# Two sums for the last three pairs of experts, and the third added earlier: one change to a fused two-layer transformer kernel on Trainium2

## The chip, the cores and the metric

The kernel runs on one core of a Trainium2 chip. The metric is the time of one execution on the device in microseconds (us), as the median of several runs. The engines are called by their short names: PE (TensorE, the matrix products), DVE (VectorE), ACT (ScalarE), POOL (GpSimd) and SP (SyncE, which here only issues DMAs). POOL also issues DMAs, the indirect ones; ACT issues a few. All data is float32.

## The reference, cut to what matters

Two transformer layers work on 2048 tokens of 512 features. Layer 0 is windowed attention and a mixture of 64 experts, of which each token uses 8; layer 1 is another windowed attention and a dense network of 2048 inner features whose weights go through Walsh-Hadamard transforms. The change lies where the experts end and layer 1 begins:

```python
# layer 0, experts: every token's rows of 8 experts are weighted and added up
y = lax.ragged_dot(hact, jnp.swapaxes(down_proj, 1, 2), group_sizes)
out = jnp.zeros_like(x).at[tok].add(y * w[:, None])
...
x = x + gb * _L0_ffn_ref(h, ...)
# layer 1 starts with a normalisation of that x
h = _layernorm(x, axis=-1) * (1 + ca) + sa
x = x + ga * _L1_attn_ref(h, ...)
```

## The kernel before, in words

**Residual and tiles.** The stream `x` stays in SBUF as `x_sb`, 16 tiles of 128 tokens by 512 features. The experts are sorted by load and taken in 32 pairs (`for q in range(NQ)`, L1104); `ROOM` (L44) says how many rows a pair's experts may hold, from 440 down to 184. Rows that do not fit go to a loop of their own behind the last pair (`tc.For_i(0, n_more, 1)`, L1149), which all engines pass, taken or not.

**One pair.** For each pair the rows are gathered by POOL (`fetch_x`, L877), transposed by PE (`x_T`, L886; its results are copied by ACT and DVE), multiplied (`gate_up`, L902, then `down`, L935), and DVE weights the result into a tile `yo` (L950, pool `ex`, 8 buffers). The weights of pair q+2 are fetched by SP while pair q is worked on (`fetch_w`, L612, from L1118).

**Sums.** The rows of an expert belong to scattered tokens. They are added in DRAM: POOL issues an indirect DMA that adds a `yo` tile of up to 128 rows onto a buffer `sums[k]` (`add_rows`, L953). Two DMAs that add onto the same buffer must not overlap, so each waits until the one before it on that buffer has landed. There are six buffers (`NSUM`, L55): the pairs 0 to 20 (up to `LATE`, L56) use the buffers 0, 1, 2 in turn, the pairs 21 to 31 use 3, 4, 5 in turn, by a running number of the add (L967):

```python
k = st_.setdefault("sum", 0)
st_["sum"] += 1
add_rows(k % 3 + (3 if q >= LATE else 0), yo, tidx[0:m, col : col + 1])
```

Over the whole kernel there are 164 adds, numbered 0 to 163 here. The pairs 28 to 31 have four each: pair 28 has the adds 148 to 151, pair 29 152 to 155, pair 30 156 to 159, and pair 31 160 to 163.

**The first three sums.** When the pairs that use them are done, SP loads them back during the pairs 22 to 29 (`earlier`, L971, called at L1110), two token tiles and six loads of 256 KB in each pair, and DVE adds them to `x_sb` one pair later (L1144). They land in buffers of the pools `h1` and `h2` (tags `wdb`, one buffer, and `wda`, two) that other work used before, and `load_proj` (L858) takes the `wda` buffers again in the last pair for layer 1's projections.

**Behind the last pair.** Two column blocks of layer 1's down weights still lack one Hadamard product: `fetch_last` (L1051) loads eight pieces, `last_products` (L1064) multiplies them on PE into the pool `p_x` (two PSUM banks), copies each into a `yo` buffer by ACT and DVE in turn, and stores it to DRAM, the even ones from ACT and the odd ones from SP. `wdo_n` is the copy of product n. Then comes the loop for rows that did not fit, at which every engine waits for all DMAs that were issued before it.

**Layer 1's start.** `rest(i)` (L1219) loads token tile i of the sums 3, 4 and 5 into a buffer (`cb`, three of them), the first two tiles partly from ACT. `summed(i)` (L1248) adds the three to `x_sb` on DVE and takes the statistics, `normal(i)` scales on ACT, and PE transposes (`across`, L1271) and projects. Tiles go in the groups of `GROUPS` (L62): two, two, four, four and four; the work on a group's sums stands between the projections of the group before it.

**What sets the order.** A scheduler of the framework places every engine's instructions; each engine then runs its own list in order, DMA issues on SP and ACT included. `tc.issue_after` (as in `in_turn`, L595) pins some of it by hand. DMAs from SP and ACT share eight completion semaphores in turn, so a DMA also waits until the eighth before it has landed.

Of the kernel before, what the change touches and what calls it, by code (L numbers as in the profile page):

```python
# [12 lines left out]
F32 = mybir.dt.float32  # L13
# [9 lines left out]
P = 128  # L23
T = 2048
NT = T // P
D = 512
# [17 lines left out]
ROOM = (  # L44
    440, 384, 352, 344, 332, 320, 312, 312, 304, 296, 292, 288, 284, 280, 276, 268,
    260, 256, 252, 252, 248, 248, 240, 240, 232, 228, 220, 220, 212, 204, 200, 184,
)
# [5 lines left out]


NSUM = 6  # L55
LATE = 21  # L56
WARM = 6
NX = 12

# [69 lines left out]
def block_kernel(ctx: ExitStack, tc: tile.TileContext, t: dict, out: bass.AP):  # L129
    nc = tc.nc  # L130
# [41 lines left out]
    wd_d = dram.tile([KC, P, FC, P], F32, tag="wd_d", name="wd_d")  # L172
    sums = [dram.tile([T + P, D], F32, tag=f"sum{k}", name=f"sum{k}") for k in range(NSUM)]
# [91 lines left out]
    with tc.tile_pool(name="a0", bufs=1) as ap, tc.tile_pool(name="a0k", bufs=1) as kp:  # L265
# [8 lines left out]
        with tc.tile_pool(name="a0h", bufs=1) as hp, tc.tile_pool(name="a0w", bufs=1) as wp, tc.tile_pool(  # L274
            name="a0n", bufs=5
# [85 lines left out]
            third = TQ // 3  # L361
            for n in range(3):
                normed_T([3 * n, 3 * n + 1, 3 * n + 2], hT, 3 * n * P, m0[1], m0[0], np_, psA, "a0")
                cols = slice(n * third, (n + 1) * third)
                ps = psA.tile([P, D], F32, tag="ps", name=f"k0_{n}")
# [5 lines left out]
                for c in range(KC):  # L371
                    ps = psA.tile([P, D], F32, tag="ps", name=f"q0_{n}_{c}")
# [9 lines left out]
            ps = psA.tile([P, 8, 64], F32, tag="ps", name="v0")  # L382
            ps2 = psA.tile([P, 64], F32, tag="ps", name="v0_8")
            left = TQ - 8 * P
            for i in range(TQT):
                n = P if i < 8 else left
                o = ps[:, i, :] if i < 8 else ps2[0:n, :]
# [5 lines left out]
            n = 0  # L393
# [26 lines left out]
        with tc.tile_pool(name="rn", bufs=4) as rn, tc.tile_pool(name="a0s", bufs=2) as sp, tc.tile_pool(name="p_s", bufs=2, space=PSUM) as p_s, tc.tile_pool(  # L420
            name="p_t", bufs=2, space=PSUM
# [204 lines left out]
    with tc.tile_pool(name="rw", bufs=1) as rw, tc.tile_pool(name="rh", bufs=3) as rh:  # L626
        with tc.tile_pool(name="p_q", bufs=3, space=PSUM) as p_q, tc.tile_pool(
# [158 lines left out]
            n = 0  # L786
# [84 lines left out]
    with tc.tile_pool(name="h1", bufs=1) as h1, tc.tile_pool(name="p_x", bufs=2, space=PSUM) as p_x, tc.tile_pool(  # L871
# [81 lines left out]
        def add_rows(k, yo, idx):  # L953
            G.indirect_dma_start(  # L954
                out=sums[k][:, :],
                out_offset=bass.IndirectOffsetOnAxis(ap=idx, axis=0),
                in_=yo,
                in_offset=None,
                compute_op=ALU.add,
            )  # L960

        def to_sums(q):
            def put(h, b, m, yo):
                col = FIRST[2 * q + h] + b
                k = st_.setdefault("sum", 0)
                st_["sum"] += 1
                add_rows(k % 3 + (3 if q >= LATE else 0), yo, tidx[0:m, col : col + 1])  # L967

            return put

        def earlier(n):  # L971

            got = []
            for i in (2 * n, 2 * n + 1):
                for k in range(3):
                    j, at = divmod(3 * i + k, 4)
                    if at == 0:
                        pool, tag = (h1, "wdb") if j % 3 == 2 else (h2, "wda")
                        st_["sa"] = pool.tile([P, 4, D], F32, tag=tag, name=f"sa_{j}")
                    part = st_["sa"][:, at, :]  # L980
                    nc.sync.dma_start(out=part, in_=sums[k][i * P : (i + 1) * P, :])
                    got.append((i, part))
            return got


# [77 lines left out]

        def last_products(got):  # L1064
            for n, (cb, c4, a) in enumerate(got):
                ps = p_x.tile([P, 4, P], F32, tag="xp", name=f"wdh_{cb}_{c4}")
                with in_turn():
                    st_["pe"] = mm(ps, had, a)
                o = ex.tile([P, D], F32, tag="yo", name=f"wdo_{n}", bufs=8).rearrange("p (c m) -> p c m", c=4)
                (V.tensor_copy if n % 2 else S.copy)(o, ps)  # L1070
                (nc.sync if n % 2 else nc.scalar).dma_start(out=wd_d[cb][:, c4 : c4 + 4, :], in_=o)


        def turn(q):
# [29 lines left out]
        for q in range(NQ):  # L1104
            if q == NQ - 1:
                n_more = nc.values_load(more[0:1, 0:1], min_val=0, max_val=MORE)
            two = [st_[2 * q], st_[2 * q + 1]]
            late = st_.pop("late", [])
            if LATE < q <= LATE + NT // 2:
                st_["late"] = earlier(q - LATE - 1)  # L1110

            def fetch(p):
                for r in (2 * p, 2 * p + 1) if p < NQ else ():
                    fetch_w(r)
                    fetch_x(r)

            if q:
                fetch(q + 2)  # L1118
            if q == NQ - 1:
                load_proj()  # L1120
                behind_it = fetch_last()
            steps = turn(q + 1) if q + 1 < NQ else []
            with in_turn():
                hA, hB, last = gate_up(
                    q, [s["w"][0] for s in two], [s["xT"] for s in two], ROOM[q], lambda: take(steps, 2),
                    lambda: take(opening, KC),
                )
            if q == 0:
                fetch(2)
            take(steps, 2)  # L1130
            if q + 1 < NQ:
                with tc.issue_after(last.ins):
                    shares(q + 1)
            for s in range(0, ROOM[q], P):

                with in_turn(), tc.issue_after(st_["gx"].ins):
                    down(q, s, [a["w"][1] for a in two], hA, hB, ROOM[q], [a["share"] for a in two], to_sums(q))
                take(steps, 2)
            take(steps, 2 * KC)
            with tc.issue_after(last.ins):  # L1140
                for _ in range(2):
                    next(side)
                for i, part in late:
                    V.tensor_tensor(x_sb[:, i, :], x_sb[:, i, :], part, ALU.add)  # L1144
# [47 lines left out]
    with tc.tile_pool(name="a1", bufs=1) as ap:  # L1192
# [7 lines left out]
        with tc.tile_pool(name="b1h", bufs=2) as hp, tc.tile_pool(  # L1200
# [18 lines left out]
            def rest(i, eng=None):  # L1219

                rests[i] = cb.tile([P, 3, D], F32, tag="sum", name=f"sum_{i}")
                for k in range(3):
                    (eng if k and eng else nc.sync).dma_start(
                        out=rests[i][:, k, :], in_=sums[3 + k][i * P : (i + 1) * P, :]
                    )

# [16 lines left out]
            def prepare(g):  # L1243

                first, n = GROUPS[g]
                norms = {}

                def summed(i):  # L1248
                    for k in range(3):
                        v_(V.tensor_tensor, x_sb[:, i, :], x_sb[:, i, :], rests[i][:, k, :], ALU.add)  # L1250
                    if i + 3 < NT:
                        rest(i + 3)
                    st = small.tile([P, 6], F32, tag="st", name=f"st_a1_{i}")
                    mv = small.tile([P, 1, 2], F32, tag="mv", name=f"mv_a1_{i}")
                    v_(V.bn_stats, st, x_sb[:, i, :])
                    v_(V.bn_aggr, mv[:, 0, :], st)
                    rs = small.tile([P, 1], F32, tag="rs", name=f"rs_a1_{i}")
                    S.activation(rs, mv[:, :, 1], AF.Sqrt, bias=eps)
                    norms[i] = mv, rs

                def normal(i):
                    mv, rs = norms[i]
                    v_(V.reciprocal, rs, rs)

                    off = small.tile([P, 1], F32, tag="off", name=f"off_a1_{i}")
                    v_(V.scalar_tensor_tensor, off, mv[:, 0, 0:1], -1.0, rs, ALU.mult, ALU.mult)
                    xn = np_.tile([P, D], F32, tag="xn", name=f"xn_a1_{i}")
                    S.activation(xn, x_sb[:, i, :], AF.Identity, bias=off, scale=rs)
                    norms[i] = xn

                def across():  # L1271
                    hT = hTs[g] = hp.tile([P, KC, D], F32, tag="hT", name=f"hT1_{g}")
                    for c in range(KC):
                        ps = psA.tile([P, D], F32, tag="ps", name=f"nT_a1_{g}_{c}")
                        for a in range(n):
                            with after("PE"):
                                prev["PE"] = TE.transpose(
                                    ps[:, a * P : (a + 1) * P], norms[first + a][:, c * P : (c + 1) * P], ident
                                )
                        o, ps = hT[:, c, 0 : n * P], ps[:, 0 : n * P]  # L1280
                        sc_, sh_ = m1[1][:, c : c + 1], m1[0][:, c : c + 1]
                        if c % 2:
                            S.activation(o, ps, AF.Identity, bias=sh_, scale=sc_)
                        else:
                            v_(V.tensor_scalar, o, ps, sc_, sh_, ALU.mult, ALU.add)

                steps = []
                for i in range(first, first + n + 1):
                    def step(i=i):
                        if i < first + n:  # L1290
                            summed(i)
                        if i > first:
                            normal(i - 1)

                    steps.append(step)
                return steps, across
# [504 lines left out]
```

## Time and profile before

| what | value |
|---|---|
| time, three runs | 2038.03, 2042.15 and 2044.28 us, median 2042.15 us |
| the profiled execution's own time | 2033.98 us |
| its span (first to last instruction) | 2032.2 us |
| PE busy in the span | 1936.8 us (95%) |
| DVE, ACT, POOL busy | 1087.7, 509.8 and 563.7 us |
| PE's idle time between the experts and layer 1 | 17.59 us, from 1031.4 to 1049.0 us |
| mean granted PE clock | 0.98 |

All stamps are microseconds from the start of the span. A line of the timeline has the start, the duration, the engine, the source line, the operation, the tiles written and read, a count, and in brackets how long the engine had been idle before it and what ended that. "L954 POOL DMA_INDIRECT" is the time in which POOL prepares an add, not its travel. The time from that stamp until the data has landed is the landing time; the view of DMAs gives it for a single add when the window holds only that one. In the view that cuts the span into windows, the last two columns are the mean busy share of the DMA engines and what they moved; a share of 1.0 means that they always had work. In the chain of waits, a line "DMA a<-b" is time in which the end was waiting for that transfer.

### The profile page before, as it was taken

How to read it: one execution, taken by the hardware profiler on the slowest of the kernel's cores; microseconds unless marked ns; L12 is line 12 of the kernel's file. 1: busy time of each engine (PE TensorE's matmuls, PEld its weight loads, DVE VectorE, ACT ScalarE, POOL GpSimd, SP SyncE). 2: the span in 40 equal slices, each digit the busy share in tenths (PEclk: the TensorE clock that was granted, in tenths of full speed). 3: DMA queues.
4: the chain of work that ended last, by engine and by line, in shares of the span. 5: the costliest groups of instructions: out<-in, count | busy, mean ns of one | idle time of the engine just before them, and what ended most of it. 6: DMA issues, size and time to landing. Idle time of an engine off the chain costs nothing.

```text
span 2032.2 us, 28791 instructions
## 1 busy us (share of the span) xinstructions
PE 1936.8 (95%) x10794; PEld 1237.7 (61%) x10794; DVE 1087.7 (54%) x2591; ACT 509.8 (25%) x1185; POOL 563.7 (28%) x438
## 2 busy tenths in 40 slices
PE   8999878999999999999968989999999999999998
PEld 4655545455555556666635555556777776777775
DVE  3566564534454443345558767766545545535443
ACT  2333323111111111111111158774111111111101
POOL 1500003575667676566531100110100010010000
PEclk9999968999999999999979999999999999999999
DMA  7790036688889899999974100004111211211210
GB/s 277 290 345 22 32 108 208 156 217 240 202 237 236 216 269 237 267 317 310 314 248 144 52 12 2 2 23 137 51 63 53 72 62 42 83 43 61 83 42 21
DMA packets 123469, 294.50 MB, mean 145 GB/s; under 512 B 21224, under 2 KB 29160, under 8 KB 120768
## 3 DMA queue, kind: packets, MB, share of 16 engines
q1 hardware_dynamic: 85424, 211.32, 30.3%
q0 software_dynamic: 36032, 77.30, 17.8%
q10 hardware_dynamic: 1872, 4.00, 0.5%
q8 instruction: 87, 1.43, 0.3%
q14 instruction: 54, 0.44, 0.1%
HBM read 212.01 MB, written 78.20 MB: 143 GB/s over the span
## 4 chain that ended last, share of the span: by engine, by line
PE 77%; DVE 8%; DMA 5%; ACT 5%; issue 1%; POOL 0%; SPq 0%; ACTq 0%; DVEq 0%; POOLq 0%
PE y L134 20%; PE p L134 18%; PE gu L134 11%; PE gub L134 5%; PE xp L893 4%; PE s L134 3%; ACT pr L1431 3%; PE po L134 2%; PE po_a L134 2%; DMA w<-in_L_gu 2%; PE pt L1376 2%; DVE x_sb L1211 1%; DMA sum<-yo,tidx 1%; PE tps L134 1%; PE o L134 1%
## 5 line engine op out<-in xcount | busy, mean ns | idle before, releaser
L954 POOL DMA_INDIRECT sum<-yo,tidx x164 | 272.3, 1660 | 112.3 <-DMA sum<-yo,tidx 41.5
L608 POOL DMA_INDIRECT xring<-h_d,tidx x164 | 181.7, 1108 | 361.4 <-PE rps L134 229.7
L134 PE MATMUL gu<-xT,w 128*128 128x312 f32 (+26 forms) x1024 | 245.2, 397 | 1.8 <-DMA w<-in_L_gu 1.8
L134 PE MATMUL y<-wd,act 128*128 128x512 f32 x512 | 230.3, 593 | 1.5 <-DVE act L1570 1.4
L134 PEld LDWEIGHTS gu<-xT,w 128*128 128x128 f32 x1024 | 189.8, 191 | 58.0 <-issue 18.3
L134 PEld LDWEIGHTS y<-wd,act 128*128 128x128 f32 x512 | 97.0, 190 | 98.0 <-issue 91.6
L896 ACT ACTIVATE xT<-xp,modc,modc 128x312 f32<-128x312 f32 (+26 forms) x128 | 74.1, 579 | 328.7 <-PE xp L893 300.4
L950 DVE SCALAR_TENSOR_TENSOR yo<-y,wc,modr 128x512 f32<-128x512 f32 (+22 forms) x164 | 116.6, 744 | 69.8 <-PE y L134 69.3
L134 PE MATMUL y<-w,hA 128*128 128x512 f32 (+22 forms) x328 | 149.5, 596 | 0.5 <-DVE yo L950 0.5
L916 DVE TENSOR_TENSOR hA<-hA,gu 128x312 f32<-128x312 f32 (+26 forms) x64 | 28.2, 440 | 189.0 <-PE xp L893 110.3
L1431 ACT ACTIVATE pr<-ng,nb 128x208 f32<-128x208 f32 (+1 forms) x256 | 115.1, 451 | 52.4 <-DVE nb L1421 52.4
L134 PE MATMUL gub<-xT,w 128*64 128x312 f32 (+26 forms) x1024 | 125.4, 398 | 0.0
L237 POOL TENSOR_TENSOR xh<-hT 128x1024 f32<-128x1024 f32 x4 | 9.4, 2361 | 416.9 <-ACT hT L1645 401.7
L134 PE MATMUL p<-xt,ws 128*128 128x256 f32 x512 | 120.9, 379 | 3.5 <-DVE ws L1570 3.5
L134 PE MATMUL p<-xt,wr 128*128 128x256 f32 x512 | 120.8, 379 | 0.0
L893 PEld LDWEIGHTS xp<-cst,xring 128*128 128x128 f32 x656 | 73.0, 142 | 73.0 <-issue 55.8
L134 PE MATMUL p<-xh,wr 128*128 128x256 f32 x512 | 116.6, 379 | 0.3 <-DVE u L1570 0.3
L134 PEld LDWEIGHTS p<-xt,ws 128*128 128x128 f32 x512 | 96.7, 190 | 27.4 <-issue 15.8
L134 PEld LDWEIGHTS p<-xt,wr 128*128 128x128 f32 x512 | 96.8, 190 | 23.6 <-issue 10.8
L893 PE MATMUL xp<-cst,xring 128*128 128x128 f32 x656 | 100.2, 284 | 6.0 <-DMA xring<-h_d,tidx 4.8
L134 PEld LDWEIGHTS p<-xh,wr 128*128 128x128 f32 x512 | 96.9, 190 | 14.3 <-DVE u L1570 0.7
L1725 ACT ACTIVATE sg<-two,L_ws_gate 128x512 f32<-128x512 f32 x32 | 23.1, 721 | 308.8 <-DVE two L1570 308.7
(384 smaller groups left out, 2957.9 us busy)
## 6 DMA issues: line engine op xcount, KB each, us to landing
w<-in_L_gu SPq DMA_DIRECT2D x64, 768.0 KB, 7.6
wr<-in_L_Wug SPq DMA_DIRECT2D x64, 512.0 KB, 4.7
sum<-xring SPq DMA_DIRECT2D x6, 4352.0 KB, 31.0
w<-in_L_dn SPq DMA_DIRECT2D x64, 256.0 KB, 8.9
sa<-sum SPq DMA_DIRECT2D x48, 256.0 KB, 10.2
sum<-sum SPq DMA_DIRECT2D x44, 256.0 KB, 3.6
w<-in_L_dn SPq DMA_DIRECT2D x64, 128.0 KB, 8.9
xring<-in_L_wmod SPq DMA_DIRECT2D x4, 1536.0 KB, 11.3
```

The costliest lines, as they stand in the source:

```text
L134: return TE.matmul(o, lhsT, rhs, start=start, stop=stop)
L237: eng.tensor_tensor(b[:, :, 0, :], a[:, :, 0, :], a[:, :, 1, :], ALU.add)
L608: return G.indirect_dma_start(out=dst, out_offset=None, in_=src[:, :], in_offset=bass.IndirectOffsetOnAxis(ap=idx, axis=0))
L893: st_["pe"] = TE.transpose(xp[:, b * P : (b + 1) * P], xg[:, c * P : (c + 1) * P], ident)
L896: S.activation(xT[:, c, 0:n], xp[:, 0:n], AF.Identity, bias=sh, scale=sc)
L916: V.tensor_tensor(o[:, 0:n], o[:, 0:n], ps[1][:, 0:n], ALU.mult)
L950: V.scalar_tensor_tensor(yo, ys[h], shares[h][rows, b : b + 1], m0[5][rows, :], ALU.mult, ALU.mult)
L954: G.indirect_dma_start(out=sums[k][:, :], out_offset=bass.IndirectOffsetOnAxis(ap=idx, axis=0), in_=yo, in_offset=None, compute_op=ALU.add,)
L1211: prev["V"] = f(*a)
L1376: prev["PE"] = f(*a)
L1431: S.activation(prs[i, c][:, j, :nk], ng[:, :nk], AF.Exp, bias=nb, scale=-1.0, accum_out=totals[i][:, c, j : j + 1],)
L1725: S.activation(sg, gate, AF.Silu, scale=wsg[:, f : f + 1])
```

## The change: a third sum that ends earlier, and five banks

The first three sums end one pair earlier (`LATE` 20 in place of 21): the pairs 0 to 19 use the sums 0 to 2, and their loads and DVE adds fall one pair earlier too. The pairs 20 to 28 use the sums 3, 4, 5 in turn. The pairs 29, 30 and 31 use only 4 and 5 in turn. Sum 3 is thereby complete after pair 28. For the token tiles 0 to 7 (`AHEAD` 8) it is loaded at the start of pair 30 (`third`, eight loads of 256 KB, into the buffers `wdb` and `wda`) and added to `x_sb` in pair 30's list of DVE adds. Layer 1 then loads and adds two sums for the tiles 0 to 7, and three for the tiles 8 to 15 as before. For the tiles 0 and 1 ACT issues one load each in place of two.

The products behind the last pair use the two banks of `p_x` and the three of `p_g` in turn. SP stores only the products 1 and 3; ACT stores the other six.

```diff
-LATE = 21
+LATE = 20
+LAST = len(ROOM) - 3
+AHEAD = 8
...
-                add_rows(k % 3 + (3 if q >= LATE else 0), yo, tidx[0:m, col : col + 1])
+                add_rows(k % 2 + 4 if q >= LAST else k % 3 + (3 if q >= LATE else 0), yo, tidx[0:m, col : col + 1])
...
+        def third():
+
+            got = []
+            for i in range(AHEAD):
+                if i % 4 == 0:
+                    pool, tag = ((h1, "wdb"), (h2, "wda"))[i // 4]
+                    part = pool.tile([P, 4, D], F32, tag=tag, name=f"sc_{i}")
+                nc.sync.dma_start(out=part[:, i % 4, :], in_=sums[3][i * P : (i + 1) * P, :])
+                got.append((i, part[:, i % 4, :]))
+            return got
...
-                ps = p_x.tile([P, 4, P], F32, tag="xp", name=f"wdh_{cb}_{c4}")
+                pool, tag = (p_g, "g") if n % 2 else (p_x, "xp")
+                ps = pool.tile([P, 4, P], F32, tag=tag, name=f"wdh_{cb}_{c4}")
...
-                (nc.sync if n % 2 else nc.scalar).dma_start(out=wd_d[cb][:, c4 : c4 + 4, :], in_=o)
+                (nc.sync if n in (1, 3) else nc.scalar).dma_start(out=wd_d[cb][:, c4 : c4 + 4, :], in_=o)
...
             if LATE < q <= LATE + NT // 2:
                 st_["late"] = earlier(q - LATE - 1)
+            if q == NQ - 2:
+                late = late + third()
...
-                for k in range(3):
-                    (eng if k and eng else nc.sync).dma_start(
+                for k in range(1 if i < AHEAD else 0, 3):
+                    (eng if k == 2 and eng else nc.sync).dma_start(
                         out=rests[i][:, k, :], in_=sums[3 + k][i * P : (i + 1) * P, :]
                     )
...
-                    for k in range(3):
+                    for k in range(1 if i < AHEAD else 0, 3):
                         v_(V.tensor_tensor, x_sb[:, i, :], x_sb[:, i, :], rests[i][:, k, :], ALU.add)
```

## The prediction

> **What bounds the kernel now.** I read the page first. PE is busy for 95% of the span, so the change can only gain where PE stands still. Then PE's timeline around the change: from 840 us, where the loads of the first three sums begin, to the last product, PE idles twice, 0.93 us at 877.89 and 0.89 us at 964.27. The one large hole is between the experts and layer 1: 17.59 us before the first transpose at 1049.01. The third view is the chain of waits through that hole. Columns are start, duration and what was waited for.
>
> ```profile
> 1025.69 5.35 DMA sum<-yo,tidx
> ...
> 1031.14 0.59 ACT wdo L1070
> ...
> 1031.75 3.16 DMA wd_d<-wdo
> ...
> 1035.64 2.22 DMA wd_d<-wdo
> ...
> 1039.23 6.90 DMA sum<-sum
> ...
> 1046.23 0.70 DVE x_sb L1211
> ...
> 1049.72 0.48 PE nT_a L1277
> ```
>
> The hole begins with a scatter add. Add 162, issued by POOL at 1025.69, lands at 1031.04. Only then is its `yo` buffer free for the copy of product 6. That copy is stored (landing 1034.91), all engines pass the loop for rows that did not fit, the last store (product 7, placed behind the loop) lands at 1037.86, and only then do the loads of the sums begin; the last load that the first two token tiles need is issued at 1039.23 and lands at 1046.14. So everything hangs on when add 162 lands. POOL's timeline shows how the adds come along; these are the adds 151 to 163:
>
> ```profile
> 989.10 2.84 POOL L954 DMA_INDIRECT sum<-yo,tidx  x1 [0.86 <-DVE x_sb L1144]
> 992.25 2.68 POOL L954 DMA_INDIRECT sum<-yo,tidx  x1 [0.30 <-DMA sum<-yo,tidx]
> 996.18 1.57 POOL L954 DMA_INDIRECT sum<-yo,tidx  x1 [1.25 <-DVE xT L898]
> 998.36 1.84 POOL L954 DMA_INDIRECT sum<-yo,tidx  x1 [0.62 <-issue]
> 1003.45 1.83 POOL L954 DMA_INDIRECT sum<-yo,tidx  x1 [3.25 <-issue]
> 1007.70 1.57 POOL L954 DMA_INDIRECT sum<-yo,tidx  x1 [2.42 <-DVE yo L950]
> 1009.98 1.57 POOL L954 DMA_INDIRECT sum<-yo,tidx  x1 [0.71 <-DVE x_sb L1144]
> 1014.14 1.51 POOL L954 DMA_INDIRECT sum<-yo,tidx  x1 [2.59 <-DMA sum<-yo,tidx]
> 1016.16 1.53 POOL L954 DMA_INDIRECT sum<-yo,tidx  x1 [0.51 <-DVE hA L916]
> 1021.92 1.59 POOL L954 DMA_INDIRECT sum<-yo,tidx  x1 [4.23 <-DVE yo L950]
> 1023.82 1.57 POOL L954 DMA_INDIRECT sum<-yo,tidx  x1 [0.30 <-issue]
> 1025.69 1.45 POOL L954 DMA_INDIRECT sum<-yo,tidx  x1 [0.30 <-DVE yo L950]
> 1027.52 1.45 POOL L954 DMA_INDIRECT sum<-yo,tidx  x1 [0.38 <-issue]
> ```
>
> The view of DMAs, one add to a window, gives landing times: 8.7 us for add 150 (issued 986.73), 10.3 for the one at 992.25, 8.4 at 996.18, 10.9 at 998.36, 9.9 at 1003.45, 7.6 at 1007.70, 7.9 at 1014.14, then 4.8, 5.6, 5.3 and 5.6 for pair 31. An add starts about 0.8 us after the add three before it has landed: 992.25 + 10.3 = 1002.55, and add 155 starts at 1003.45; 1003.45 + 9.9 = 1013.35, and add 158 starts at 1014.14. So in pairs 29 and 30 the adds are already held by their own landing, and three sums just keep up: three adds in about 11 us, four in 14 to 15, while a pair takes PE some 16 us (its gate products start at 977.97, 994.11 and 1010.09). Why landing takes so long shows in the windows, whose last two columns are the DMA engines' share and GB/s:
>
> ```profile
> 990.00:1000.00 10.00, 10.00 (x54) 7.39 (x52) 5.84 (x11) 1.71 (x4) 7.83 (x4) 1.00 1.06 327
> 1010.00:1020.00 10.00, 10.00 (x73) 8.12 (x73) 2.52 (x6) 1.47 (x4) 4.59 (x3) 1.00 1.05 304
> 1020.00:1030.00 10.00, 10.00 (x26) 2.83 (x24) 4.74 (x7) 1.76 (x3) 6.06 (x4) 1.00 0.95 215
> ```
>
> The DMA engines always have work until 1020; then the load falls, and with it the landing time.
>
> **The two sums.** From pair 29 on, an add waits for the add two before it. The even adds, 152 to 162, become one chain on sum 4, behind add 151, which is on sum 4 too and landed near 997.6 (0.8 before add 154 started). I walk the chain with the landing time of the row nearest in time, and 0.8 us for each turn. Add 152 starts at 998.4 and takes 10.9, landing at 1009.3. Add 154 starts at 1010.1, takes 7.7, lands at 1017.8. Add 156: 1018.6, about 6.3 (between 7.9 at 1014.14 and 4.8 at 1021.92), 1024.9. Add 158: 1025.7, 5.3, 1031.0. Add 160: 1031.8, 5.5, 1037.3. Add 162: 1038.1, 5.5, 1043.6. Before it was 1031.04, so the hole ends **12.6 us** later, since the way from there to the loads (copy, store, loop, last store) is unchanged. The bounds: with every add's own landing time from before (10.3, 10.9, 7.6, 7.9, 4.8, 5.3; together 46.8, and 4.8 of turns) it lands at 1049.2, 18 us later. If instead the landing time is the adds queueing behind each other, two in flight need two thirds of it, not below 4.8: 7.3, 5.2 and four times 4.8, with the turns 36.5, landing at 1034.1, 3 us later.
>
> Here the Trainium skill speaks against my sum, and for the change. "DMA: Bandwidth & Descriptors", section "Anatomy of one DMA — SWDGE (gpsimd) path", gives a DMA issued by GpSimd about 2.0 us plus its bytes over 436 GB/s; that would be an estimated 2.6 us for 256 KB. By it a turn takes 3.4 us, six turns 20.4, the chain would be done before the last `yo` exists, and two sums cost nothing. The rows say 4.8 to 12.8 us for these adds in pairs 24 to 31, with the DMA engines full. I take the rows.
>
> **What layer 1 saves at its start.** Nine loads of 256 KB for the first three tiles become six, and ACT issues one add-in load per tile. The last load that tile 1 needs goes out about one 0.45 us issue earlier and has fewer in front of it: the loads issued at 1038.2 landed in 4.3 us, that of 1039.23 in 6.9. Tile 1 would be there by 1042.7, and then DVE sets the pace: from 1041.5, two adds of 0.69, statistics 0.9, two adds, statistics, instead of what ended at 1047.7. That is **1.6 us**. For the tiles 2 to 7 six more DVE adds go, 0.72 us each with its gap, 4.3 us. DVE is the limit there (18.3 of the 20 us from 1060 to 1080, 16.4 of the next 20), and PE waits for it, 1.94 us at 1060.19, then 0.77, 1.60, 2.88 and 1.27 us from 1074.77 to 1089.47; between 1064.5 and 1074 PE is the limit and the gain of tiles 2 and 3 is mostly lost. I take 0.7 for those two and 2.9 for the other four, **3.6 us**. Bounds for both together: 3 (only two stretches count) and 8 us (adds beside POOL's work took up to 1.65, and PE's clock, 0.83 from 1080 to 1100, recovers).
>
> **The loads of `third`.** The first four need sum 3 whole, that is add 150 landed (986.73 + 8.7 = 995.4), and the buffer `wdb`, free after pair 29's DVE adds at 993.5. On SP they stand ahead of the weights of pair 31 and of layer 1's projections; the other four stand around those weights. Together 5.2 MB from the first to the last of `third` (2.1, weights 2.4, projections and angles 0.8), with some 0.9 MB of adds, at the 310 GB/s of these rows: about 20 us, so the last lands near 1014. DVE takes this second lot first, and behind it in its list stand pair 30's `yo` and the copies that PE needs for pair 31. Before, that place on DVE (1004.26) was 7.2 us ahead of the last of these copies (1011.5); so this one ends near 1021, and the second expert's products, which began at 1012.7, start some 8.5 us late, and all behind them. What hides it is the chain: add 160, whose `yo` was there at 1021.6 and would be near 1030, does not start before 1031.8, and add 162 not before 1038.1. I take **0**, with 2 us of cover left; if the chain is fast this is what is late next, up to 7 us. The two more DVE adds of this pair (1.4 us) lie in the same wait.
>
> **The rest.** The shift by one pair moves SP's wait for the first sums to a longer pair; the stall of 0.93 at 877.89 may go or come back: 0, from -0.9 to 1. Five banks free PE from the wait of 1.2 us that each product had for a copy, but the copy of product 6 waits for add 162 and not for PE: 0; if that cover went, about 1 us of gain. Storing on ACT costs issues of 0.33 us beside waits: 0 to 0.4.
>
> **The sum.** 12.6 - 1.6 - 3.6 = 7.4 us more. The profiled execution took 2033.98 us (span 2032.2), so it would take 2041.4. The median of the runs is 2042.15, 8.2 above that execution; the same difference gives **2049.6 us**.
>
> **The rivals.** *Landing shrinks with fewer adds in flight.* The chain then costs 3 us, and the savings are 6.5 with the clock's part: 3.4 us faster, 2038.7, and up to 7 faster with all of the savings. For it speaks that pair 31's adds land in 5; against it, that the first add of a busy stretch takes as long as the third. The point of decision: the change breaks even if the chain's six landings are 5.7 us in the mean (mine are 6.9). *The third sum comes too late.* If the last of its loads lands after 1016, PE and not the chain is late, and at 1023 it adds 7 us: 2056.6. For it speaks that 1014 is near; against it, that the shift empties the DMA queues before pair 30.
>
> **How the numbers follow.** A measurement of this kernel tells about 0.3% (6 us) from no change. The two-sum chain as walked, 2045 to 2055: 0.52, of which 0.37 is slower by more than 6 us and 0.15 within. Shrinking landing times: 0.27, of which 0.15 within and 0.12 faster. A late third sum: 0.21, slower. Together slower 0.58, same 0.30, faster 0.12. Range 2037 to 2060; by itself the likeliest case has 2045 to 2055.
>
> **What would show it.** Right: POOL's even adds from 152 on start 0.8 us after the even add before has landed; pair 31's last add starts after 1036; PE's hole grows from 17.6 us although PE ends pair 31 late; DVE's adds for tiles 2 to 7 are two each, and PE's waits there shrink. Wrong: landing times under 6 us in pairs 29 and 30, or a hole under 16 us.

## The result, and the profile after

The changed kernel took 2059.44 us (median of four runs, 2057.97 to 2062.55), the kernel before 2043.22 us (four runs, 2038.03 to 2044.92). The ratio is 1.0081, with a 95% interval of 1.0057 to 1.0104: slower by 16.6 us, from 11.6 to 21.2. The forecast was 7.4 us more, with 2037 to 2060 as its range and 2045 to 2055 as its likeliest case. The direction held. The size is more than twice the forecast's, and the median lies 0.6 us inside the upper end of the range, past the likeliest case. Below, "us slower" is always a ratio's excess times the median of the kernel before on the same chip, with the interval of the ratio behind it.

The two profiled executions differ more than that, by 28.6 us (2062.55 against 2033.98): that of after is the slowest of its four and that of before the fastest. 4.9 us of it are there at the first expert product already (346.34 against 341.48), ahead of all that the change touches. So the traces are read for places, and the experiments for sizes.

The places first. These groups of the page of after name two waits of PE. The column behind the bar is busy time and mean ns, and the last one is the idle time just before the group and what ended it:

```profile
L956 POOL DMA_INDIRECT sum<-yo,tidx x164 | 274.9, 1677 | 129.1 <-DMA sum<-yo,tidx 62.1
L136 PE MATMUL gu<-xT,w 128*128 128x312 f32 (+26 forms) x1024 | 248.5, 401 | 8.5 <-DMA w<-in_L_gu 8.5
...
L136 PE MATMUL y<-w,hA 128*128 128x512 f32 (+22 forms) x328 | 150.5, 599 | 14.1 <-DVE yo L952 14.1
```

Before, the same three groups had been idle for 112.3 us (41.5 of them for an add to land), 1.8 us and 0.5 us. POOL waits 20.6 us longer for adds, which was forecast. PE's 8.5 us for weights and 14.1 us for DVE were not: they are two stalls among the experts, where the kernel before had none above 0.93 us.

The first stall, in the chain of waits of after (start, duration, what):

```profile
831.90 11.32 DMA sum<-yo,tidx
...
846.73 10.52 DMA sa<-sum
...
857.26 14.03 DMA w<-in_L_gu
...
871.34 6.40 PE gu L136 x16
```

SP's timeline of after, around the first of these stamps, and PE's timeline of before at its largest stall:

```profile
838.38 9.01 SPq L983 DMA_DIRECT2D sa<-sum  x8
```

```profile
877.89 3.51 PE L134 MATMUL gu<-xT,w 128*128 128x240 f32 x16 [0.93 <-DMA w<-in_L_gu]
```

Read the chain from the bottom. PE's products of pair 22's second expert start at 871.34, 7.51 us after the product before them had ended, because their weights were only issued at 857.26, when the eighth DMA before them (the load of 846.73) had landed. They stood on SP behind twelve loads of the first three sums. The first of these waited 10.1 us for the third add of pair 19, which was issued at 828.03 and landed in 10.3; it went at 838.38. The second could not go before pair 19's last add, issued at 831.90, had landed at 843.22. In the lists of SP's waits from 825 to 880 us these are the rows of after and of before (total, times, longest):

```profile
SPq L983 <- DMA sum<-yo,tidx: 14.6, 2, 10.1
```

```profile
SPq L981 <- DMA sum<-yo,tidx: 7.6, 3, 3.4
```

Those 16 products then took 6.40 us; the same shape took 3.41 us at 860.42. The granted PE clock had fallen to 0.85 from 860 to 870 and 0.64 from 870 to 880, so this stall cost some 3 us more behind its end.

The second stall and the hole, in the same view; these lines answer to those of before:

```profile
1025.13 8.48 DMA sc<-sum
...
1034.92 0.76 DVE yo L952
...
1035.72 3.95 PE y L136 x6
...
1052.59 4.89 DMA sum<-yo,tidx
...
1058.28 5.26 DMA sum<-yo,tidx
...
1063.62 0.59 ACT wdo L1084
```

At 1035.72 PE has stood for 13.56 us. It waits for a `yo` that stands on DVE behind adds of the third sum, and DVE waits for the loads of that sum: 13.7 us in three waits, 7.3 the longest. The last of these waits ends when the load issued at 1025.13, the seventh of the eight, lands at 1033.61. Only behind it comes what the forecast was about: the adds of pair 31, each behind the add two before it, with add 162 landing at 1063.54, and the copy at 1063.62. From the last store's landing (1070.36) to the first transpose (1080.10) it is 9.74 us, against 11.15 before. The hole is 18.60 us, hardly more than the 17.59 of before, because PE itself came so late.

POOL's timeline of after shows the chain on sum 4; the four lines are the adds 152, 154, 160 and 162:

```profile
1012.80 1.58 POOL L956 DMA_INDIRECT sum<-yo,tidx  x1 [3.59 <-DMA sum<-yo,tidx]
...
1023.02 1.84 POOL L956 DMA_INDIRECT sum<-yo,tidx  x1 [6.77 <-DMA sum<-yo,tidx]
...
1052.59 1.59 POOL L956 DMA_INDIRECT sum<-yo,tidx  x1 [5.92 <-DVE yo L952]
...
1058.28 1.45 POOL L956 DMA_INDIRECT sum<-yo,tidx  x1 [2.23 <-DMA sum<-yo,tidx]
```

Add 152 landed in 9.3 us, at 1022.1, and add 154 started 0.9 us later. Add 160 landed in 4.9, at 1057.5, and add 162 started 0.8 later. That is the walk of the forecast. But add 160 waited for its `yo`, so up to there the chain was no longer what came last.

### The profile page after: what moved, and what is told of

Same layout as the page of the kernel before. It is cut to its first block, busy times and chain, and to the rows that moved or that the text cites. A ratio compares the mean times of both kernels' runs of the same rounds, so it can differ in the third digit from the quotient of the medians.

```text
span 2060.8 us, 28784 instructions
## 1 busy us (share of the span) xinstructions
PE 1945.7 (94%) x10794; PEld 1244.2 (60%) x10794; DVE 1086.4 (53%) x2591; ACT 509.7 (25%) x1185; POOL 568.0 (28%) x438
## 4 chain that ended last, share of the span: by engine, by line
PE 76%; DVE 7%; DMA 7%; ACT 4%; issue 1%; SPq 0%; POOL 0%; DVEq 0%; ACTq 0%; POOLq 0%
PE y L136 19%; PE p L136 18%; PE gu L136 10%; PE gub L136 5%; PE xp L895 3%; PE s L136 3%; DMA w<-in_L_gu 3%; ACT pr L1447 3%; PE po_a L136 3%; PE po L136 3%; PE pt L1392 2%; DMA sum<-yo,tidx 1%; DVE x_sb L1227 1%; DMA sa<-sum 1%; PE tps L136 1%
## 5 line engine op out<-in xcount | busy, mean ns | idle before, releaser
L136 PE MATMUL y<-w,hA 128*128 128x512 f32 (+22 forms) x328 | 150.5, 599 | 14.1 <-DVE yo L952 14.1
```

What stands on the lines that cost most here:

```text
L136: return TE.matmul(o, lhsT, rhs, start=start, stop=stop)
```

## The experiments

The theory after this reading (A): the cost is a sum of parts, namely the shift (SP waits for pair 19's adds with pair 22's weights queued behind), the chain on two sums, and the third sum's late loads, less what layer 1 saves. Its rivals: the shift only moves a wait that costs nothing, the chain is harmless, or all of it is a difference between executions.

**The kernel before once more, unchanged.**

> The kernel before, unchanged, for a second profile. Its first profile was 8 to 11 us below its other times, and the profile of the change 3 us above its own. If chance lies in what comes ahead of the change (the experts began 4.9 us later in the profile of the change, at 346.3 us) or in the stall at the first sums (0.93 us before, 7.51 us in the change), this profile shows other values there: first expert product between 341 and 347 us, stall between 1 and 8 us, hole between experts and layer 1 again near 17.6 us.

One run: 2038.96 us. Its first expert product came at 344.75, there was no stall above 0.32 us in the pairs 22 to 31, and the hole was 19.98 us. So 3 us at the first product and 2 us in the hole are differences between executions of one program; in this repeat nothing like a stall of 7 or 13 us appears.

**The shift alone.**

```diff
-LATE = 21
+LATE = 20
```

> Only the shift of the first sums by one pair. Theory A (three costs: shift, chain of two sums, third sum's loads): SP waits for pair 19's last adds, which landed in 11.6 and 11.7 us in the profile before (pair 20's in 7.4 to 8.4), with the weights of pair 22 queued behind; PE stalls some 7 us there, plus 3 us at a lower clock, so 5 to 9 us slower. Theory B (the shift is free, as the prediction took it): within 2 us of before, and the 7.5 us stall was chance.

Ratio 1.0030 (1.0020 to 1.0041): 6.1 us slower (4.1 to 8.4). Its PE timeline has the stall of after:

```profile
868.03 5.07 PE L134 MATMUL gu<-xT,w 128*128 128x240 f32 x16 [6.82 <-DMA w<-in_L_gu]
```

SP waited for these adds as long as in after, 12.0 us in two waits, the longest 10.1. The shift is not free.

**Two sums for the pairs 29 to 31 alone.**

```diff
-                add_rows(k % 3 + (3 if q >= LATE else 0), yo, tidx[0:m, col : col + 1])
+                add_rows(k % 2 + 4 if q >= LAST else k % 3 + (3 if q >= LATE else 0), yo, tidx[0:m, col : col + 1])
```

> Only the two sums for the last three pairs; sum 3 is still loaded and added for all tiles at layer 1's start, no shift, old banks. Theory A: the chain of even adds ends 10 to 14 us later than before with nothing saved, so 10 to 14 us slower, POOL waiting for the add two before it, PE's hole 28 to 32 us. Theory C (two sums are free by themselves; the third sum's loads made the loss by holding DVE and PE in pair 30): within 2 us of before, hole near 18 us.

Ratio 1.0045 (1.0026 to 1.0064): 9.2 us slower (5.3 to 13.1). POOL's timeline of this kernel, the adds 152, 154, 158, 160 and 162:

```profile
996.78 1.58 POOL L955 DMA_INDIRECT sum<-yo,tidx  x1 [6.37 <-DMA sum<-yo,tidx]
...
1007.94 1.89 POOL L955 DMA_INDIRECT sum<-yo,tidx  x1 [7.71 <-DMA sum<-yo,tidx]
...
1025.83 1.51 POOL L955 DMA_INDIRECT sum<-yo,tidx  x1 [1.69 <-issue]
...
1030.82 1.59 POOL L955 DMA_INDIRECT sum<-yo,tidx  x1 [1.22 <-DMA sum<-yo,tidx]
...
1036.80 1.45 POOL L955 DMA_INDIRECT sum<-yo,tidx  x1 [1.74 <-DMA sum<-yo,tidx]
```

The even adds from 152 on landed in 10.3, 11.5, 4.9, 4.2, 5.2 and 3.8 us, and each next one started 0.7 to 0.9 us behind. This is the chain as walked. The hole itself was 18.34 us and not 28 to 32 as expected, because PE stood already among the products behind the experts (0.57 to 1.66 us, six times, for copies that wait for the buffers of adds). So the whole stretch is compared: from the first product behind the experts to the first transpose it took 37.74 us in this trace, against 25.32 in before's and 27.69 in the repeat's.

**The change without the third sum's early loads** (shift, two sums and banks; three sums at layer 1's start).

```diff
-AHEAD = 8
+AHEAD = 0
...
-            if q == NQ - 2:
-                late = late + third()
```

> The whole change without the third sum's early loads and adds (layer 1 loads and adds three sums for all tiles): shift, two sums and five banks. Theory A: shift plus chain, 15 to 22 us slower than before; the change itself, with the stall of pair 30 but with 5 us of savings, was 16 slower, so this is no faster than it. Theory C: near the shift alone, 0 to 9 us slower, and clearly faster than the change.

Ratio 1.0079 (1.0056 to 1.0103): 16.2 us slower (11.4 to 21.1), as much as the change. Layer 1 saves nothing here. So the third sum gives the change nothing on balance, within intervals of some 5 us either way: by the medians, what it saves at layer 1's start it costs elsewhere, and the trace of after has a stall in pair 30 to show for it.

**The savings alone** (sum 3 of the tiles 0 to 7 is left out).

```diff
-                for k in range(3):
-                    (eng if k and eng else nc.sync).dma_start(
+                for k in range(1 if i < AHEAD else 0, 3):
+                    (eng if k == 2 and eng else nc.sync).dma_start(
...
-                    for k in range(3):
+                    for k in range(1 if i < AHEAD else 0, 3):
```

> The kernel before, except that layer 1 does not load and add sum 3 for the tiles 0 to 7: that part of the result is left out. It gives what the change saves at layer 1's start, with nothing paid for it. Theory A (the forecast's size): 5.2 us faster than before, of it 1.6 in the way from the last store of the products behind the experts to the first transpose (11.15 us in the trace of before), and the rest in PE's waits for DVE behind it. Theory C (PE sets the pace there anyway, or the last load of the other two sums lands as late as before): less than 2 us faster. Expected by the bounds given: 3 to 8 us faster.

Ratio 0.9971 (0.9959 to 0.9983): 5.9 us faster (3.5 to 8.4). The forecast's 5.2 stands, and theory C (less than 2) falls.

**The third sum's loads without their wait for add 150.**

```diff
-                nc.sync.dma_start(out=part[:, i % 4, :], in_=sums[3][i * P : (i + 1) * P, :])
+                nc.sync.dma_start(out=part[:, i % 4, :], in_=sums[0][i * P : (i + 1) * P, :])
```

> The change, except that the eight loads of the third sum read sum 0, which was complete ten pairs before, and not sum 3: the same loads, buffers and adds, without the wait for add 150 (sum 0 is added twice for eight tiles and sum 3 not at all, so that part of the result is another one). Theory A1 (the stall of pair 30, 13.56 us in the trace of the change, comes from loads that wait for sum 3 to be complete): they go out at 998 to 1000 in place of 1010, the stall goes below 3 us, and the whole is 11 to 12 us slower than before, 4 to 5 better than the change. Theory A2 (the stall comes from 2 MB more in queues that are full, and from adds placed ahead of pair 30's on DVE): the loads leave earlier but land as late, the stall stays above 8 us, and the whole stays at +15 to +17.

Ratio 1.0062 (1.0041 to 1.0083): 12.7 us slower (8.4 to 17.0), an interval that overlaps that of the change. The first loads went out at 995.94 and no longer waited for an add. PE still stood:

```profile
1033.65 1.98 PE L136 MATMUL y<-w,hA 128*72 128x512 f32 x2 [8.84 <-DVE yo L952]
```

SP's list mixes these loads with the weights of pair 31 and of layer 1, and the last three still went out at 1021.47, the last landing at about 1032. Between these two traces the wait for sum 3 makes at most 4.7 of the 13.56 us; the rest is left to where the loads stand on SP and their adds on DVE. Theory A1's bound of 3 us for the stall was missed, and A2's stall above 8 us came. The time lies nearer to A1's 11 to 12 us than to A2's 15 to 17, but its interval holds both.

**The third sum's adds one pair later on DVE.**

```diff
-                late = late + third()
+                st_["late"] = third()
```

> The change, with the eight loads of the third sum as they are, but their eight adds on DVE one pair later (pair 31, behind its gate products). Theory A (PE's stall of 13.56 us in pair 30 is DVE waiting for these loads with pair 30's results queued behind it): the stall goes, pair 31's adds start when the add two before has landed, and the whole is 3 to 6 us better than the change, +10 to +13. Theory A2 (the loads' volume itself holds the weights of pair 31): PE waits for weights in place of DVE, and the whole stays near +16. Theory A3 (the adds only move the wait into pair 31, where DVE must give its last results to the adds): +14 to +18 with a stall of the last adds behind the loads.

Ratio 1.0067 (1.0043 to 1.0092): 13.7 us slower (8.8 to 18.8). The time does not tell it from the change; the trace does. The wait for DVE in pair 30 is gone, and PE's only stall there is for weights:

```profile
1025.46 4.07 PE L136 MATMUL gu<-xT,w 128*128 128x184 f32 x16 [2.29 <-DMA w<-in_L_gu]
```

The hole is 27.14 us in this trace, 8.5 more than in after's, where the stall had gone down by 11.3. So most of what the stall gave back, the hole took.

**Five banks and ACT's stores alone** (the change of `last_products`, without the rest).

> The kernel before with nothing but the last part of the change: the products behind the experts in five banks, and six of their eight stores from ACT. The forecast says 0 (0 to 0.4 slower by the issues on ACT, the gain of 1 us hidden behind the copy that waits for add 162); the time from add 162's landing to the first transpose stays near 18 us. Rival (stores on ACT stand before copies of ACT, and hold them): 1 to 3 us slower.

Ratio 1.0005 (0.9994 to 1.0015): 1.0 us slower (-1.2 to 3.1). No effect can be told; 0 and 0.4 are both inside. The eight products took 7.73 us in the trace of before and 7.13 here, so what five banks free is 0.6 us in all.

**The shift, with the loads left in the pairs 22 to 29.**

```diff
-LATE = 21
+LATE = 20
...
-            if LATE < q <= LATE + NT // 2:
-                st_["late"] = earlier(q - LATE - 1)
+            if 21 < q <= 21 + NT // 2:
+                st_["late"] = earlier(q - 22)
```

> The kernel before with the first three sums ended one pair earlier (pairs 0 to 19), as in the change, but with their loads left in the pairs 22 to 29, where they stood. The change of that number alone, loads moved too, was 6.1 us slower. Theory A (the 6 us are SP's first load waiting for pair 19's slowly landing adds with weights queued behind it): no wait of SP above 2 us at these loads, no stall of PE for weights near 870, and 0 to 1 us faster than before. Theory B (the 6 us come from where the adds lie, pair 20's now on the other sums): still some 5 us slower, with SP not waiting.

Ratio 1.0036 (1.0023 to 1.0048): 7.4 us slower (4.7 to 9.8). The time alone would speak for theory B, but the trace shows that the edit did not do what was meant: SP still waited 10.0 us at these loads, and PE stood 6.39 us at 874.33. The scheduler had put the loads ahead of pair 22's weights all the same. So moving the call by one pair left the loads where they were; by what rule the scheduler places them, no run shows. This experiment decides nothing between the theories, and the next one pins the order.

**The shift, with the loads pinned behind the weights.**

```diff
-LATE = 21
+LATE = 20
...
-                    nc.sync.dma_start(out=part, in_=sums[k][i * P : (i + 1) * P, :])
+                    with tc.issue_after(st_["fetched"].ins):
+                        nc.sync.dma_start(out=part, in_=sums[k][i * P : (i + 1) * P, :])
```

> The kernel before with the first three sums ended one pair earlier, and the loads of these sums pinned on SP behind the weights of the pair after the one that calls them, which is where they stood in the kernel before (behind the second expert's weights of pair 22). In the run meant to do this before, the scheduler had put the loads in the same place ahead of pair 22's weights, and SP waited 10.0 us as in the change. Theory A (the shift's 6 us are weights queued behind a load that waits for pair 19's adds): SP waits less than 2 us for these adds, PE does not stand at its products of pair 22, and the time is that of before, from 2 us faster to 2 us slower. Theory B (the adds of pair 20 on the other sums cost it): 5 to 7 us slower still.

Ratio 1.0002 (0.9992 to 1.0012): 0.4 us slower (-1.6 to 2.5). SP's timeline of this kernel shows the second expert's weights of pair 22 ahead of the first six loads:

```profile
843.32 0.34 SPq L618 DMA_DIRECT2D w<-in_L_gu  x1
...
845.04 6.70 SPq L982 DMA_DIRECT2D sa<-sum  x6
```

SP's wait for the adds is 0.4 us, and PE has no stall between 815 and 940. The sums of pair 20's adds are the same as in the run of the shift alone; only the order on SP differs, for all the loads of the pairs 22 to 29. The 6 us were the order, within the 2.5 us of this interval, and theory B (5 to 7 us) falls.

**Copies that wait for no add.** The forecast read the hole as hanging on add 162 by way of product 6's copy.

```diff
-                o = ex.tile([P, D], F32, tag="yo", name=f"wdo_{n}", bufs=8).rearrange("p (c m) -> p c m", c=4)
-                (V.tensor_copy if n % 2 else S.copy)(o, ps)
-                (nc.sync if n % 2 else nc.scalar).dma_start(out=wd_d[cb][:, c4 : c4 + 4, :], in_=o)
+                (V.tensor_copy if n % 2 else S.copy)(a, ps)
+                (nc.sync if n % 2 else nc.scalar).dma_start(out=wd_d[cb][:, c4 : c4 + 4, :], in_=a)
```

> The kernel before, except that the products behind the experts are copied back into the loaded tile that PE has just read, and not into a buffer that an add still reads. It tests the reading of the hole on which the forecast stands: everything hangs on add 162 by way of product 6's copy. If so (theory A), no copy waits for an add, all stores are out some 3 us earlier, and only the landing of adds 162 and 163 is left ahead of the loads: 2 to 4 us faster than before. If the last store (placed behind the loop) or the adds themselves end last anyway (theory C): less than 1 us faster.

Ratio 0.9995 (0.9979 to 1.0011): 1.0 us faster (-2.3 to 4.3, below nothing a loss). From the last add's issue to the first load of the sums it is now 7.30 us, against 10.35 before and 12.33 in the repeat, so the copies did wait. But in this trace the last add went out 7.65 us after the first product behind the experts, against 3.83 and 3.88, and from that product to the first transpose it is 27.68 us, as in the repeat. The loads need the last adds landed anyway: add 163 landed at 1043.6 here, and the first load went at 1044.81. A gain of 2 to 4 us is not shown, nor shut out.

**The change with both orders mended**: all loads of the sums pinned behind the weights, and the third's adds in pair 31.

```diff
+                    with tc.issue_after(st_["fetched"].ins):
+                        nc.sync.dma_start(out=part, in_=sums[k][i * P : (i + 1) * P, :])
...
+                with tc.issue_after(st_["fetched"].ins):
+                    nc.sync.dma_start(out=part[:, i % 4, :], in_=sums[3][i * P : (i + 1) * P, :])
...
-                late = late + third()
+                st_["late"] = third()
```

> The change with its two stalls taken out by order alone: the loads of the first three sums and those of the third sum are pinned on SP behind the weights that were fetched last when they are called, and the third's adds on DVE come in pair 31. What is left are the two-sum chain and what layer 1 saves. Theory A (the change is a sum of separate parts: shift 6, chain 9, savings -6, the rest the third's stall): no wait of PE above 3 us in the pairs 22 to 31, and 3 us slower than before (9.2 - 5.9), from 0 to 7; the forecast's own sum without stalls was 7.4. Theory B (the parts are not separate: the 2 MB of the third's loads lengthen the landing of the last adds wherever they stand): 10 us slower or more.

Ratio 1.0024 (1.0013 to 1.0035): 4.9 us slower (2.7 to 7.2). The stalls at 871 and 1035 are gone. What is left is the hole, 26.91 us ahead of the first transpose at 1063.29. The chain of waits of this trace leads through it from an add of pair 31, number 161:

```profile
1036.25 7.91 DMA sum<-yo,tidx
```

Its landing at 1044.16 lets a copy go (1044.29), and stores, loads and sums follow.

PE's largest stall in the pairs 22 to 31 is 3.21 us, just above the 3 expected, for a `yo` at 979.37; the time is inside the 0 to 7 of theory A. No version came out faster than the kernel before beyond its interval, but for the one that leaves adds out.

## Why the prediction was right in direction and half in size

The parts, as forecast and as measured alone:

| part | forecast, us | measured, us |
|---|---|---|
| two-sum chain | +12.6 (3 to 18) | +9.2 (5.3 to 13.1) |
| layer 1's start, tiles 0 to 7 | -5.2 (-3 to -8) | -5.9 (-3.5 to -8.4) |
| five banks, ACT's stores | 0 (to 0.4) | +1.0 (-1.2 to 3.1) |
| shift by one pair | 0 (-0.9 to 1) | +6.1 (4.1 to 8.4) |
| the third's loads and adds | 0 (up to 7) | about +6, by difference |
| whole | +7.4 | +16.6 (11.6 to 21.2) |

The last part is 16.6 less the four above it, 10.4. Each carries its interval, and taken as independent they make about 7 us either way. So the times alone do not show that this part is above nothing; the stall of 13.56 us in the trace does show that the cover failed. Two sums check the table. Shift, chain and banks make 16.3, and the change without the third was measured at 16.2. Chain, savings and banks make 4.3, and the change with both stalls mended came to 4.9. The forecast had 7.4 for just that.

**The chain: right, with a median below the forecast.** The step "Add 162: 1038.1, 5.5, 1043.6" is close to what the run with two sums alone shows. There add 162 starts at 1036.80, with a first expert product 1.19 us earlier than in the trace of before, so 1038.0 on that trace's clock. It lands in 3.8 in place of 5.5. The six landings have a mean of 6.7 us, where the forecast had 6.9 and the point of decision of the first rival lay at 5.7. Landing did not shrink with fewer adds in flight where the rival needed it: the first two took 10.3 and 11.5 us, and 10.3 and 10.9 in the trace of before with three sums. The weighing against the Trainium skill ("DMA: Bandwidth & Descriptors", "Anatomy of one DMA — SWDGE (gpsimd) path") came out for the rows: the estimate of 2.6 us made from it was exceeded by every one of the six, 3.8 to 11.5.

**The savings: right.** Of the 1.6 us ahead of the first transpose the trace of after shows 1.4 (11.15 to 9.74). The other 3.6 came as 4.4 to 4.8: from the first transpose to the same later block of 13 transposes it takes 38.04 us in after, 42.80 in before and 42.45 in the repeat.

**The shift: the step that failed.** "The shift by one pair moves SP's wait for the first sums to a longer pair; the stall of 0.93 at 877.89 may go or come back: 0, from -0.9 to 1." The wait was seen, and its price was taken from PE's stall of 0.93 us, that is from a place where the loads stood behind all the weights of pair 22 and ahead of pair 23's. What was not asked is how long the load waits in the changed kernel, and what is queued behind it then. It was pair 22's weights, and the longest wait was 10.1 us where it had been 3.4. The size could have been worked out: in the trace of before, pair 19's last two adds landed in 11.6 and 11.7 us, those of pair 20 in 7.4 to 8.4, so with pair 19 as the last the sums are complete some 4 us later within their pair, and the loads that wait for them come a whole pair earlier, when pair 22's weights are still to be fetched. The run with the loads pinned shows that the order is the whole of it, within 2.5 us. The traces of all runs say the same. In the six that have the shift unpinned, PE stood 3.28 to 7.51 us for weights at pair 22's second expert. In the six without the shift it stood 0 to 3.26 us at pair 23's. With the slower products behind a stall counted in, the means are 8.0 and 2.1 us, and their difference of 5.9 is near the 6.1 measured.

**The third sum: a cover that was too thin.** The forecast took 0 with 2 us of cover, and put the last load's landing near 1014, to be compared with 1016. Its own start, 995.4, and its 20 us make 1015.4, so the cover was 0.6 us by its own figures. On the clock of before (pair 30's gate products started at 994.11 there and at 1008.47 in after, 14.4 later) the last load that DVE waited for landed at 1019.2. The loads started at 995.9, as foreseen (add 150 landed at 995.4 there), but up to that landing it took 23.3 us and not about 20. The last three loads went out 14.2 us behind the first, and from 1010 to 1020 on after's own clock the DMA engines moved 253 GB/s (share 0.87), where the forecast took 310 throughout. So the second rival, "the third sum comes too late", holds as a mechanism, with a price of about 6 where it gave 7. That its 2056.6 came near the measured 2059.44 is in part luck: it rests on a chain of 12.6, 3.4 more than measured, and on a shift of nothing, 6.1 less.

**The banks.** The forecast's "wait of 1.2 us that each product had for a copy" is not in the trace of before, where the eight products follow each other in 7.73 us; as the part was taken at 0, nothing hung on it.

**What stays open.** How much of the third's 6 us is the wait for sum 3 and how much the place on SP and DVE: in traces 4.7 of 13.56 is the most that the first can be, but the times of those runs overlap. Whether the chain costs 9 or 12 is inside its interval.

## What to carry to other kernels

When a wait is moved on an in-order queue, read what stands behind the waiting instruction in the new order, as built, and not the stall that the wait made at its old place: the same loads cost 6 us ahead of pair 22's weights and 0.4 behind them. Where the order is a scheduler's, moving a call in the program may move nothing: pin it, and read the order in the trace. And when a cost is taken at nothing because something else ends later, put a size on the error of both ends: two parts taken at nothing came to some 12 us, and only because the chain was put 3 too high is the forecast no more than 9 us short.

## What the runs showed of the hardware that had not been expected

A stall of PE can be paid for again behind it, and the runs show behind which lengths it was. At the second expert of the pairs 22 and 23 the same 16 products took 3.51 us behind stalls of 0.57, 0.93 and 1.51 us (the runs of two sums alone, before and the savings alone). They took 5.1 to 6.4 us behind eight stalls of 2.56 to 7.51 us; behind the shortest of these, in the run with copies that wait for no add, the granted clock was 0.59 from 881.4 to 884.0. Lengths between 1.51 and 2.56 us did not occur. In after the granted clock was 0.64 from 870 to 880, behind 7.51 us of standing, and 0.50 from 1030 to 1040, around the end of the 13.56 us:

```profile
1020.00:1030.00 10.00, 2.15 (x10) 0.64 (x6) 0.69 (x1) 0.50 (x1) 3.67 (x2) 0.87 1.07 310
1030.00:1040.00 10.00, 4.28 (x8) 1.09 (x9) 5.91 (x10) 0.00 (x0) 3.70 (x2) 0.50 0.86 244
```

In these windows of after the third column from the end is the granted clock, and ahead of it stand the busy times of PE, weight loads, DVE, ACT and POOL.

The landing time of an add onto DRAM did not go with how many adds were in flight. In the trace of before, with up to three in flight, pair 31's adds took 4.8 to 5.6 us. In the run with two sums alone, never more than two in flight from add 152 on, the adds 152, 154 and 155 took 10.3, 11.5 and 11.7, and later ones 3.5 to 5.2. Nor did it go with the engines' share alone: it was 0.72 on average while add 155 travelled (1010.1 to 1021.8), and 1.04 for add 162 of before, which took 5.3. What goes with it in these two traces is how many DMAs of SP and ACT were on their way when the add was issued: seven or eight for the adds from 148 on that took 7.6 us and more, none to three for those that took 5.6 and less. That is no rule: in the run with both orders mended add 160 took 10.2 us with one or two on their way.
